# A new instruction order with a refitted plan, first weights loaded by pairs of heads, and q's inverse norm moved into the local exponential

## The chip, the cores and the metric

The kernel runs on one core of one Trainium2 chip. The metric is the device time of one execution in microseconds; the runs of a kernel are summed up by their median.

## The reference

The input is x of shape (8, 512, 128) in fp32: eight independent sequences. Cut to what matters, the reference computes

```python
# 1. causal attention, 16 heads of 64, keys and values shared by pairs of heads
scores = q @ k / 8, causal mask; z = softmax(scores) @ v
x = layernorm(x + z @ W_out + b_out)
# 2. two layers (DEPTH = 2); x1 is the input of the first
for l in range(2):
    h = shift_token(x)                    # second half of the channels one token late
    q, k, v = split(h @ wqkv[l])          # 8 heads of 64
    q = q / |q| * q_scale; k = k / |k| * k_scale     # l2norm per head and token
    q, k = rotary_xpos(q, k)              # also scaled by QK_SCALE = 8
    o = local attention: windows of 64 queries, 128 keys, softmax
    x = x + o @ wo
    h = layernorm(shift_token(x)) * lg + lb
    a, g = split(h @ w1 + b1); x = x + (a * gelu(g)) @ w2 + b2
out = layernorm(x1 + x)
```

The inverse norm of q is one number for each token and head. It is a positive factor of a whole row of scores, so softmax(n * s) can be computed as exp(n * s - max(n * s)) with n applied before the rotary step, or after the scores.

## The kernel before, in words

Everything is fp32, except the mask's small bf16 matmuls. One sequence is held transposed, channels on partitions and 512 tokens along the free axis, in tiles of 128 tokens (NT = 4). The work is written as some 5,900 small operations, each a Python closure with an engine, a planned time and the buffers it reads and writes. `Plan.run` issues them one after the other in `ORDER`, a list of operation numbers written out in the file; each engine gets its instructions in that order. While it does so it keeps a model of the time, and from that model alone it chooses which slot of a buffer class an operation gets: eight PSUM banks, 21 tiles of class `two`, 11 of `four`, 7 of `small` and so on. `HOP` and `TAIL` are the model's delays between an operation and those that wait for it. The waits that the program contains come from the data and the slots; the model's times are not in the program.

Attention (`attention`): for each pair of key heads (`gp`, four of them) `heads` projects keys (L828), queries (L834, two of them) and values (L843); for each of two query heads `results` computes the scores of four query tiles in three groups (L883, two heads side by side on 64 rows each). For each group and head the DVE adds the mask and takes the extreme (`least`, L895), ACT exponentiates with the extreme as a per-partition bias (L907), the DVE inverts the sums (L915), and POOL normalizes (`normalize`, L922). The weights are then transposed on PE (L935, copied back by ACT, L942) or, for most groups of all sequences but the first ("far"), by a DVE transpose in 32 x 32 blocks (L957) and two DMA steps through DRAM (`leave` and `come`, L800 and L804, issued by SP). `values` (L976) multiplies with v on 64 columns for each head, L985 copies back, and `project_out` (L995) adds the heads.

The two layers (`layer`): for each tile of 128 tokens, v (L1033, copied by ACT at L1036 and shifted by windows at L1042 on POOL); q and k (L1056), squared by ACT straight from the bank (L1063), summed by DVE (L1066); the inverse norms by POOL and ACT (L1071, L1077, L1078, and `newton`, L1085 to L1088). The DVE reads the same banks for the rotary step (L1102, L1109), POOL adds the two parts (L1116, 128 x 1024 for q and k together) and multiplies q and k by their inverse norms (`over_norms`, L1122, twice 128 x 512). They are turned by the DVE and DMA (L1156, then SP) or, for the last sequence ("quick"), by PE and ACT (L1136, L1143). Scores of a tile: mask and products in one bank for each parity of heads (L1183, L1198, on quarters of the PE array); for each of the two halves the greatest by DVE (L1219), four exponentials by ACT (L1224), the reciprocals by DVE (L1230), the normalization by POOL (L1232), a transpose on PE (L1239) and a copy by ACT (L1242). Then the outputs (L1251, copied at L1259), wo (L1264), the residual (L1270), layernorm (L754 to L786, L1278), and the gated block (L1288, L1295, L1303, L1306, L1313, L1319). L1328 adds x1, and L1331 stores.

The attention of one sequence and the layers of earlier ones are interleaved in `ORDER`, so that PE has other work while a softmax runs on the other engines. In the plan an operation on PE has one of four tile modes (whole array, rows, columns, quadrants), and a change of mode is planned at 0.1 us. For the last sequence nothing is left to interleave with its second layer.

At the start the loads of `w_k` and `w_v` as a whole and half of `w_q` are issued by ACT's queue (L620 to L623), the other half of `w_q` (`got_q`, L610) and x (L615) by SP's queue, which then issues the tables and the later weights.

Of the kernel before, what the change touches and what calls it, by code (L numbers as in the profile page):

```python
# [12 lines left out]
ALU = mybir.AluOpType  # L13
# [10 lines left out]
class Buf:  # L24


    __slots__ = ("cls", "view", "slot", "t", "left", "free", "marks")

    def __init__(self, cls=None, view=None):
        self.cls, self.view = cls, view  # L30
        self.slot = self.t = None
        self.left = 0
        self.free = 0.0
        self.marks = {}


class Op:
    __slots__ = ("eng", "us", "lat", "fn", "bufs", "mode", "needs", "then", "n", "need", "ready")


class Plan:
# [4 lines left out]
    HOP = (0.055, 0.034, 0.034, 0.085, 0.05)  # L46
# [10 lines left out]
    def op(self, eng, us, fn, r=(), w=(), lat=0.0, hold=(), mode=WHOLE):  # L57
# [33 lines left out]
        o.bufs = bufs  # L91
        self.ops.append(o)

    def run(self, order):
# [6 lines left out]
        for n in order:  # L101
            o = self.ops[n]
            assert not o.need, "an operation stands before one that it needs"
            ready = o.ready
            now = max(at[o.eng], ready)
# [20 lines left out]
            o.fn()  # L126
            for d in o.then:
                d.need -= 1
                d.ready = max(d.ready, end + self.HOP[d.eng])
# [8 lines left out]
    0, 66, 67, 258, 68, 76, 1, 82, 2, 12, 69, 7, 78, 77, 11, 13, 6, 9, 8, 10, 63, 80, 79, 83, 174,  # L138
    175, 187, 200, 194, 259, 808, 81, 215, 188, 16, 176, 177, 201, 195, 228, 241, 189, 207, 208, 32,
    28, 181, 190, 170, 235, 202, 216, 182, 56, 222, 203, 229, 223, 224, 191, 166, 178, 204, 49, 236,  # L140
    19, 183, 209, 184, 179, 210, 74, 171, 237, 180, 14, 196, 242, 230, 168, 72, 185, 225, 211, 3,
    226, 248, 238, 167, 197, 231, 73, 70, 192, 217, 218, 198, 169, 75, 27, 193, 199, 232, 186, 212,
    243, 233, 249, 2262, 219, 71, 220, 205, 206, 221, 172, 234, 173, 213, 244, 239, 250, 245, 240,
    251, 252, 53, 246, 18, 247, 138, 139, 227, 145, 40, 253, 22, 140, 125, 141, 142, 126, 46, 214,
    151, 158, 254, 127, 128, 143, 809, 132, 146, 159, 147, 152, 153, 129, 43, 110, 4, 144, 50, 97,
    160, 161, 148, 84, 154, 64, 111, 262, 104, 133, 134, 21, 155, 130, 135, 255, 47, 98, 85, 149,
    51, 810, 99, 86, 91, 92, 100, 162, 136, 263, 163, 156, 41, 87, 131, 137, 105, 117, 150, 106,
    260, 118, 157, 101, 93, 813, 119, 88, 112, 102, 89, 90, 103, 94, 164, 107, 113, 814, 95, 120,
    121, 122, 114, 115, 116, 108, 292, 165, 96, 52, 299, 109, 266, 293, 300, 267, 301, 294, 268,
    279, 286, 302, 295, 296, 123, 287, 280, 273, 303, 124, 320, 288, 289, 333, 307, 281, 23, 274,  # L150
    304, 269, 20, 270, 282, 327, 25, 297, 334, 335, 321, 322, 290, 291, 314, 275, 323, 283, 5, 276,
    315, 328, 44, 336, 340, 324, 256, 341, 325, 308, 329, 330, 316, 317, 284, 277, 309, 326, 271,
    310, 337, 342, 343, 278, 298, 331, 338, 272, 318, 344, 311, 332, 261, 285, 2989, 257, 305, 319,
    312, 345, 17, 45, 313, 339, 415, 422, 65, 423, 389, 306, 390, 416, 424, 59, 346, 402, 348, 396,
    391, 392, 24, 374, 425, 409, 417, 397, 393, 410, 403, 398, 418, 361, 29, 811, 55, 15, 355, 404,
    347, 349, 399, 419, 57, 362, 411, 412, 356, 357, 358, 405, 394, 264, 350, 375, 406, 413, 351,
    368, 363, 265, 395, 369, 352, 420, 58, 426, 427, 407, 815, 400, 414, 376, 364, 365, 370, 381,
    421, 359, 408, 816, 353, 371, 372, 401, 377, 812, 382, 366, 367, 428, 383, 378, 384, 373, 354,
    379, 380, 385, 61, 360, 62, 839, 844, 840, 386, 387, 827, 832, 866, 429, 388, 841, 878, 845,
    846, 842, 847, 60, 828, 833, 883, 884, 867, 885, 879, 868, 54, 871, 430, 829, 48, 42, 843, 848,  # L160
    872, 830, 1535, 26, 831, 851, 431, 38, 873, 834, 432, 880, 881, 823, 835, 890, 849, 886, 858,
    859, 882, 433, 852, 853, 825, 434, 897, 860, 861, 1536, 874, 909, 824, 898, 1537, 869, 435, 862,
    436, 870, 821, 437, 438, 887, 836, 891, 899, 888, 900, 439, 819, 854, 447, 892, 837, 37, 850,
    838, 875, 445, 893, 826, 855, 894, 876, 901, 456, 455, 453, 820, 454, 457, 910, 485, 889, 863,
    448, 561, 487, 446, 486, 562, 36, 488, 449, 856, 857, 895, 817, 450, 493, 489, 877, 902, 496,
    822, 525, 913, 451, 533, 490, 495, 914, 452, 458, 818, 864, 494, 918, 527, 526, 896, 491, 915,
    865, 937, 916, 497, 459, 919, 925, 944, 460, 920, 903, 534, 945, 930, 926, 528, 529, 563, 921,
    927, 440, 946, 931, 938, 904, 939, 964, 952, 461, 492, 463, 917, 928, 922, 441, 932, 976, 965,
    969, 966, 929, 911, 933, 947, 970, 934, 957, 1540, 530, 531, 566, 958, 977, 912, 907, 498, 948,
    971, 978, 983, 564, 959, 923, 967, 940, 532, 953, 972, 954, 535, 536, 968, 979, 935, 481, 565,  # L170
    905, 949, 2263, 955, 960, 499, 956, 462, 924, 908, 936, 464, 980, 941, 984, 906, 973, 482, 572,
    974, 961, 537, 538, 1541, 471, 567, 568, 942, 981, 569, 521, 943, 985, 950, 982, 465, 2264, 575,
    472, 574, 573, 962, 1001, 986, 473, 474, 1006, 501, 466, 467, 1025, 539, 522, 468, 1013, 951,
    1007, 987, 444, 570, 442, 500, 975, 1032, 995, 443, 963, 988, 484, 1002, 475, 541, 1008, 476,
    1003, 469, 1018, 1019, 1014, 1004, 1015, 1016, 1009, 1005, 1552, 989, 1026, 1020, 503, 470, 996,
    1017, 502, 990, 477, 1021, 1033, 1010, 1052, 540, 1022, 1053, 1034, 543, 1064, 1071, 478, 576,
    1040, 1054, 1057, 1023, 1065, 1058, 504, 511, 1059, 1045, 1538, 542, 1055, 1066, 1041, 571, 577,
    479, 1072, 991, 1073, 1011, 1056, 1027, 1028, 505, 1029, 480, 1042, 1035, 1043, 1067, 1060,
    1046, 1047, 523, 1539, 1061, 578, 1036, 512, 1048, 1074, 993, 1037, 1553, 1030, 994, 544, 513,
    1024, 1044, 1049, 1031, 545, 1012, 524, 483, 506, 551, 1038, 1062, 992, 514, 546, 552, 1079,  # L180
    1080, 1081, 1084, 1103, 553, 1068, 1091, 1085, 580, 507, 1092, 1093, 1050, 1063, 1104, 1082,
    1051, 31, 547, 1086, 1087, 1105, 999, 579, 508, 1546, 35, 515, 1069, 1083, 1110, 1070, 1075,
    997, 582, 1076, 1096, 1106, 1097, 1077, 1000, 516, 509, 1098, 1094, 1095, 1088, 1039, 998, 1118,
    1078, 1142, 510, 1089, 1099, 1100, 1101, 1123, 1130, 1111, 1119, 517, 554, 1124, 1135, 1107,
    1108, 1547, 581, 1112, 1125, 1126, 1136, 1131, 1542, 1113, 1149, 1143, 1120, 1132, 1144, 1543,
    1090, 1724, 555, 1109, 1102, 1121, 1122, 1114, 1133, 1636, 1550, 1137, 30, 1115, 1145, 1134,
    1127, 556, 1128, 1146, 1147, 1138, 1139, 1725, 518, 1148, 1140, 1150, 583, 584, 1116, 1551,
    1554, 590, 1151, 591, 1578, 592, 1555, 1129, 548, 1117, 1566, 1637, 585, 593, 1579, 1152, 1556,
    1634, 1153, 1585, 1544, 1635, 1154, 594, 1141, 1155, 1567, 1568, 586, 1557, 1558, 1559, 1569,
    549, 1605, 1571, 1560, 1572, 1570, 1586, 595, 1561, 1562, 1593, 1563, 1545, 1587, 1573, 1574,  # L190
    1156, 1610, 1575, 1594, 1580, 1617, 550, 587, 1581, 1618, 1588, 1624, 1625, 1598, 1599, 1564,
    1157, 1626, 1576, 39, 1565, 1158, 1582, 1583, 1600, 1595, 1596, 1611, 1589, 1590, 1606, 588,
    1159, 1601, 1612, 519, 1160, 589, 1607, 557, 1584, 596, 1577, 558, 1161, 33, 1597, 1613, 1162,
    1591, 1163, 1691, 1619, 520, 1164, 1608, 1602, 1592, 1627, 1609, 1614, 1603, 1679, 1166, 1615,
    1696, 1165, 1692, 1703, 1680, 597, 1693, 1620, 559, 1174, 1697, 1694, 1684, 1685, 560, 1695,
    1698, 1172, 1173, 1704, 1181, 1621, 1681, 1699, 598, 1175, 1686, 599, 1700, 1604, 1710, 1622,
    1548, 601, 1628, 600, 1167, 602, 1682, 1687, 1182, 1705, 1683, 1616, 1623, 1629, 1183, 603,
    1208, 1180, 1214, 1711, 1688, 1689, 1176, 604, 1712, 605, 1168, 1630, 1549, 1212, 1209, 1184,
    1177, 1631, 1652, 1215, 1701, 1702, 1664, 1640, 1178, 1213, 1653, 1690, 1706, 1654, 606, 1657,
    1179, 1658, 1671, 1672, 1641, 1185, 607, 1659, 1660, 1655, 1642, 1645, 1656, 1632, 1713, 1248,  # L200
# [300 lines left out]
def kernel(  # L501
# [120 lines left out]
    for j in range(2):  # L622
        nc.scalar.dma_start(out=wq_sb[:, :, 1, j, :], in_=wq_v[:, :, 1, j, :])  # L623
# [775 lines left out]
```

## Time and profile before

| | before |
|---|---|
| median of 3 runs | 1193.21 us (1191.84 to 1193.32) |
| the profiled execution | 1189.79 us |
| its span, first to last instruction | 1188.0 us |
| granted clock of PE, share of full speed | 0.997 |
| PE busy | 1154.2 us, 97% |
| DVE, ACT, POOL busy | 952.6, 959.6 and 891.4 us (80%, 81%, 75%) |
| DMA | 173.23 MB, mean 146 GB/s |
| first and last matmul | start at 4.90 us, end at 1180.7 us |

The profiled execution lies 2 us below the fastest of the three runs, so differences are made within the profile and then applied to the median. A row of the groups gives line, engine, operation and tiles, then the busy time and the mean of one instruction in ns, then the idle time of its engine just before it and what ended that. A row of the timeline gives start, length and the merged instructions. Instructions on one engine overlap in part, so the distance from start to start is shorter than the length that is shown.

### The profile page before, as it was taken

To read this page: it belongs to the slowest core of one execution; us is meant where nothing else is said; L and a number is where in the kernel's file an instruction comes from. 1 tells how busy PE (TensorE), PEld (TensorE's weight loads), DVE (VectorE), ACT (ScalarE), POOL (GpSimd) and SP (SyncE) were. 2 spreads that over 40 slices of the span, in tenths; PEclk is the share of its full clock that TensorE was granted. 3 is DMA by queue.
4 is the path that set the end of the run, shared out by engine and by line. 5 is a ranking of instruction groups with operands and counts; after the bars stand their busy time and mean duration, and the time that the engine had idled before them with its cause. 6 is when DMAs were issued, how large, how long until landed. Compare 5 with 4: busy or idle time off the path is not lost.

```text
span 1188.0 us, 32813 instructions
## 1 busy us (share of the span) xinstructions
PE 1154.2 (97%) x11024; PEld 769.2 (65%) x11024; DVE 952.6 (80%) x2988; ACT 959.6 (81%) x3049; POOL 891.4 (75%) x1391
## 2 busy tenths in 40 slices
PE   8999999999999999999999999999999999999986
PEld 5775667566676667666576656766666676666672
DVE  3669967989887989888887888887889888968645
ACT  6867888888888878886898777887788887888783
POOL 3557955789777868778797579786879789989782
PEclk9999999999999999999999999999999999999998
DMA  7004775556655446555556535565456455203100
GB/s 190 15 2 146 241 246 156 178 178 191 196 166 178 162 140 200 174 145 170 160 172 179 188 127 168 159 190 159 157 179 194 136 161 170 81 2 109 36 2 27
DMA packets 180387, 173.23 MB, mean 146 GB/s; under 512 B 25682, under 2 KB 150780, under 8 KB 180220
## 3 DMA queue, kind: packets, MB, share of 16 engines
q1 hardware_dynamic: 178876, 170.35, 46.0%
q8 instruction: 89, 1.46, 0.5%
q10 hardware_dynamic: 1344, 0.79, 0.2%
q14 instruction: 78, 0.64, 0.2%
HBM read 88.22 MB, written 82.84 MB: 144 GB/s over the span
## 4 chain that ended last, share of the span: by engine, by line
PE 75%; DVE 7%; ACT 6%; DMA 4%; POOL 3%; SPq 2%; issue 2%; POOLq 0%; DVEq 0%; ACTq 0%
PE bank L883 11%; PE bank L976 10%; PE bank L1056 6%; PE bank L1251 4%; PE bank L1198 4%; PE bank L995 4%; PE bank L935 4%; PE bank L1264 4%; PE bank L1033 4%; PE bank L1239 4%; PE bank L834 3%; PE bank L1313 3%; PE bank L1303 3%; PE bank L1288 3%; SPq L804 2%
## 5 line engine op out<-in xcount | busy, mean ns | idle before, releaser
L922 POOL TENSOR_SCALAR p<-p,small 128x384 f32<-128x384 f32 (+3 forms) x512 | 264.9, 531 | 123.4 <-DVE small L915 91.8
L1224 ACT ACTIVATE weights<-bank,small 128x128 f32<-128x128 f32 x512 | 181.6, 383 | 27.2 <-DVE small L1219 25.8
L907 ACT ACTIVATE p<-bank,small 128x384 f32<-128x384 f32 (+1 forms) x224 | 142.4, 643 | 29.8 <-DVE small L895 22.4
L1116 POOL TENSOR_TENSOR four<-four,four 128x1024 f32<-128x1024 f32 x64 | 151.4, 2367 | 12.8 <-DVE four L1109 5.4
L1232 POOL TENSOR_TENSOR weights<-weights,small 128x512 f32<-128x512 f32 x128 | 132.3, 1039 | 37.6 <-DVE small L1230 30.3
L883 PE MATMUL bank<-four,four 64*128 64x384 f32 (+3 forms) x1024 | 160.1, 446 | 0.2 <-ACT four L985 0.2
L895 DVE CUSTOM_DVE_ANT_0 bank<-bank,cmask 128x384 f32<-128x384 f32 (+1 forms) x224 | 136.6, 635 | 25.2 <-PE bank L883 24.9
L907 ACT ACTIVATE p<-p,small 128x128 f32<-128x128 f32 (+3 forms) x288 | 135.7, 480 | 15.1 <-DVE small L895 14.8
L1122 POOL TENSOR_TENSOR four<-four,small 128x512 f32<-128x512 f32 x128 | 131.4, 1048 | 2.8
L957 DVE STREAM_TRANSPOSE p<-p 128x768 f32<-128x768 f32 (+1 forms) x112 | 122.4, 1100 | 10.5 <-POOL p L922 10.3
L1056 PE MATMUL bank<-wqkv_sb,hT 128*128 128x512 f32 x256 | 128.3, 601 | 0.2 <-ACT four L1063 0.2
L895 DVE CUSTOM_DVE_ANT_0 p<-bank,cmask 128x256 f32<-128x256 f32 (+3 forms) x288 | 97.4, 380 | 25.2 <-PE bank L883 23.8
L883 PEld LDWEIGHTS bank<-four,four 64*128 64x128 f32 x1024 | 82.8, 186 | 50.9 <-issue 17.1
L1224 ACT ACTIVATION_READ_ACCUMULATOR weights<-bank,small 128x1 f32 x512 | 114.1, 223 | 0.0
L1219 DVE TENSOR_REDUCE small<-bank 128x4 f32<-128x512 f32 x128 | 84.8, 680 | 23.7 <-PE bank L1198 17.6
L1109 DVE TENSOR_TENSOR four<-bank,tb 128x256 f32<-128x256 f32 x256 | 94.6, 414 | 11.4 <-ACT four L1063 6.7
L1102 DVE TENSOR_TENSOR four<-bank,ta 128x512 f32<-128x512 f32 x128 | 85.8, 679 | 13.9 <-ACT four L1063 9.3
L1156 DVE STREAM_TRANSPOSE four<-four 128x512 f32<-128x512 f32 x112 | 92.6, 909 | 2.3 <-POOL four L1122 2.3
L1063 ACT ACTIVATE four<-bank 128x512 f32<-128x512 f32 x128 | 75.4, 610 | 20.2 <-DVE four L1102 7.5
L1242 ACT COPY weights<-bank 128x512 f32<-128x512 f32 x128 | 74.0, 598 | 16.6 <-PE bank L1239 13.6
L1042 POOL COPY two<-two 64x512 f32<-64x512 f32 x128 | 77.2, 606 | 8.9 <-ACT two L1036 2.5
L1066 DVE TENSOR_REDUCE small<-four 128x8 f32<-128x512 f32 x128 | 80.5, 672 | 3.0 <-ACT four L1063 3.0
(104 smaller groups left out, 2692.9 us busy)
## 6 DMA issues: line engine op xcount, KB each, us to landing
dram<-p SPq DMA_DIRECT2D x56, 512.0 KB, 3.4
p4T<-dram SPq DMA_DIRECT2D x224, 128.0 KB, 3.0
dram<-four SPq DMA_DIRECT2D x112, 256.0 KB, 2.8
dram<-p SPq DMA_DIRECT2D x56, 384.0 KB, 2.7
p3T<-dram SPq DMA_DIRECT2D x224, 96.0 KB, 2.8
eight<-dram SPq DMA_DIRECT2D x224, 64.0 KB, 2.2
two<-dram SPq DMA_DIRECT2D x224, 64.0 KB, 2.3
two<-in_L_attn_resid_dram SPq DMA_DIRECT2D x8, 256.0 KB, 3.5
```

Source lines behind the costliest of these rows:

```text
L883: nc.tensor.matmul(s[j].t[:, ds(o, nk)], qT.t[ts(j, E), r, ts(t, P)], kv.t[ts(j, E), 0, :nk], start=True, stop=True,)
L895: nc.vector.tensor_tensor_reduce(s.t[:, :nk] if far else p.t[:, j, ds(o, nk)], s.t[:, ds(o, nk)], cmask[:, S - nk : S], 1.0, 3.0e38, ALU.a ...
L907: nc.scalar.activation(v, negated(p, s, j, o, nk), AF.Exp, bias=st.t[:, 2 * j + i : 2 * j + i + 1], scale=-1.0, accum_out=st.t[:, 8 + 2 * ...
L922: nc.gpsimd.tensor_scalar(v, v, st.t[:, 16 + 2 * j + i : 17 + 2 * j + i], 1.0, ALU.mult, ALU.mult,)
L957: op(DVE, 0.06 + 0.0021 * used, lambda p=p, flat=flat: nc.vector.transpose(flat(p), flat(p)), r=[p], w=[p])
L976: nc.tensor.matmul(pz.t[ts(j, E), ts(t, P)], kv.t[:, 1, ds(kb * P + j * E, E)], turned[:, j, kb] if far else p.t[:, j, ds(POFF[t] - POFF[f ...
L1056: nc.tensor.matmul(pq.t, hT.t[:, ts(t, P)], w if quick else w.rearrange("d (h e b) -> d e h b", e=2, b=B), start=True, stop=True,)
L1109: nc.vector.tensor_tensor(u[:, a], v[:, 1 - a], tb[:, l, t, s, ts(1 - a, B)].unsqueeze(1).broadcast_to([P, H, B]), ALU.mult,)
L1116: op(POOL, 2.35, lambda sw=sw, qn=qn: nc.gpsimd.tensor_tensor(qn.t, qn.t, sw.t, ALU.add), r=[qn, sw], w=[qn])
L1122: nc.gpsimd.tensor_tensor(split(qn.t[:, ts(s, HE)]), split(qn.t[:, ts(s, HE)]), y.unsqueeze(1).unsqueeze(3).broadcast_to([P, 2, H, B]), AL ...
L1224: nc.scalar.activation(weights()[:, c], s.t[:, ts(c, P)], AF.Exp, bias=part(0)[:, c : c + 1], accum_out=part(8)[:, c : c + 1],)
L1232: op(POOL, 1.05, lambda weights=weights, part=part: nc.gpsimd.tensor_tensor(weights(), weights(), spread(part(16)), ALU.mult), r=[(p, j), ...
```

## The change

Five things change in the file.

1. `ORDER` is a new list (6,015 operations for 5,889, as some are split). In the plan, `HOP` is larger (PE 0.1 for 0.055), several planned times are refitted, and a bank remembers who has read or written it and until when (`seen`): an operation of another engine on this bank is planned only after that. `Plan` uses this for its times, and so for the choice of slots.
2. There are 16 slots of class `small` for 7.
3. The first weights are loaded by pairs of heads. ACT's queue loads only the first pair's part of `w_k`, `w_q` and `w_v`; SP's queue loads the rest, eight loads for two, and the projections of a pair wait for their own parts.
4. `over_norms` on POOL treats k alone. q stays without its inverse norm; `greatest` multiplies the negated maximum of the scores (128 x 4) by the norms on the DVE, and the exponential takes the norm as a per-partition `scale` beside its per-partition `bias`. The planned time of the four exponentials stays 1.38.
5. The sum on POOL, and the DVE's transpose of q and k, are planned as two operations, one for q and one for k. The transposes were two instructions already; the sum becomes two.

```diff
-    HOP = (0.055, 0.034, 0.034, 0.085, 0.05)
+    HOP = (0.1, 0.044, 0.044, 0.09, 0.06)
...
+            for b in o.banks:
+                for eng, end in b.seen:
+                    if eng != o.eng:
+                        ready = max(ready, end + self.HOP[o.eng])
...
+            for b in o.banks:
+                b.seen.append((o.eng, end))
...
-    slots("small", [P, 64], 7)
+    slots("small", [P, 64], 16)
...
-    nc.scalar.dma_start(out=wk_sb, in_=w_k)
-    nc.scalar.dma_start(out=wv_sb, in_=w_v)
+    nc.scalar.dma_start(out=wk_sb[:, 0:2, :], in_=w_k[:, 0:2, :])
     for j in range(2):
-        nc.scalar.dma_start(out=wq_sb[:, :, 1, j, :], in_=wq_v[:, :, 1, j, :])
-    got_q = [load(wq_sb[:, :, 0, j, :], wq_v[:, :, 0, j, :], nc.sync) for j in range(2)]
-
+        nc.scalar.dma_start(out=wq_sb[:, 0, :, j, :], in_=wq_v[:, 0, :, j, :])
+    nc.scalar.dma_start(out=wv_sb[:, 0:2, :], in_=w_v[:, 0:2, :])
+    got_q = [[] for gp in range(NGP)]
+    got_q[1] = [
+        load(wk_sb[:, 2:, :], w_k[:, 2:, :], nc.sync), load(wv_sb[:, 2:, :], w_v[:, 2:, :], nc.sync)
+    ]
+    for gp in range(1, NGP):
+        got_q[gp] = got_q[gp] + [
+            load(wq_sb[:, gp, :, j, :], wq_v[:, gp, :, j, :], nc.sync) for j in range(2)]
...
-            op(POOL, 2.35, lambda sw=sw, qn=qn: nc.gpsimd.tensor_tensor(
-                qn.t, qn.t, sw.t, ALU.add), r=[qn, sw], w=[qn])
+            for s in range(2):
+                op(POOL, 1.18, lambda s=s, sw=sw, qn=qn: nc.gpsimd.tensor_tensor(
+                    qn.t[:, ts(s, HE)], qn.t[:, ts(s, HE)], sw.t[:, ts(s, HE)], ALU.add),
+                   r=[(qn, s), (sw, s)], w=[(qn, s)])
...
             def over_norms(sm=sm, qn=qn, split=split):
-                for s in range(2):
-                    y = sm.t[:, ds(32 + s * H, H)]
-                    nc.gpsimd.tensor_tensor(
-                        split(qn.t[:, ts(s, HE)]), split(qn.t[:, ts(s, HE)]),
-                        y.unsqueeze(1).unsqueeze(3).broadcast_to([P, 2, H, B]), ALU.mult,
-                    )
+                k = split(qn.t[:, HE:])
+                nc.gpsimd.tensor_tensor(
+                    k, k, sm.t[:, 32 + H : 32 + 2 * H].unsqueeze(1).unsqueeze(3).broadcast_to(
+                        [P, 2, H, B]), ALU.mult,
+                )
...
-                op(DVE, 0.6, lambda s=s[j], part=part: nc.vector.tensor_reduce(
-                    part(0), by_head(s), AX.X, ALU.max, negate=True), r=[s[j]], w=[(st, j)])
+                def norm_of(c, j=j, sm=sm):
+                    return sm.t[:, 32 + 2 * c + j : 33 + 2 * c + j]
...
+                def greatest(s=s[j], part=part, j=j, sm=sm):
+                    nc.vector.tensor_reduce(part(0), by_head(s), AX.X, ALU.max, negate=True)
+                    nc.vector.tensor_tensor(
+                        part(0), part(0),
+                        sm.t[:, 32 : 32 + H].rearrange("p (c j) -> p j c", j=2)[:, j], ALU.mult)
...
-                            bias=part(0)[:, c : c + 1], accum_out=part(8)[:, c : c + 1],
+                            bias=part(0)[:, c : c + 1], scale=norm_of(c),
+                            accum_out=part(8)[:, c : c + 1],
```

## The prediction

> **What bounds the kernel now.** First the page: busy shares, slices, chain.
>
> ```profile
> PE 1154.2 (97%) x11024; PEld 769.2 (65%) x11024; DVE 952.6 (80%) x2988; ACT 959.6 (81%) x3049; POOL 891.4 (75%) x1391
> PE   8999999999999999999999999999999999999986
> PE 75%; DVE 7%; ACT 6%; DMA 4%; POOL 3%; SPq 2%; issue 2%; POOLq 0%; DVEq 0%; ACTq 0%
> ```
>
> TensorE is the bound: it is idle for 33.8 us of 1188.0. The change removes no matmul, and both programs hold 3266 rows of matmuls in the listing of the order. All it can move is idle time, mode changes and late starts on PE. The windows say where the idle time lies:
>
> ```profile
> core 0: us, PE busy (x) PEld busy (x) DVE busy (x) ACT busy (x) POOL busy (x), PEclk, DMA share, GB/s
> 0.00:30.00 30.00, 24.43 (x143) 15.86 (x145) 11.22 (x53) 18.38 (x50) 9.79 (x26) 1.00 0.78 191
> 30.00:560.00 530.00, 524.73 (x4993) 352.52 (x4991) 439.89 (x1448) 435.70 (x1394) 392.18 (x647) 1.00 0.52 161
> 560.00:1100.00 540.00, 533.41 (x5178) 354.05 (x5174) 453.77 (x1349) 448.97 (x1443) 437.29 (x653) 1.00 0.47 149
> 1100.00:1160.00 60.00, 54.73 (x675) 39.95 (x675) 32.77 (x90) 47.16 (x154) 46.60 (x63) 1.00 0.04 12
> 1160.00:1188.00 28.00, 16.95 (x48) 6.85 (x46) 14.93 (x51) 9.38 (x11) 5.57 (x5) 0.88 0.10 29
> ```
>
> PE's idle time (length less busy time) is 5.6 us in the first stretch, 5.3 and 6.6 in the two long ones, 5.3 while only the last batch is left, and 11.0 in the last 28 us, where one serial chain runs out. But "busy" hides late starts, which the timeline shows:
>
> ```profile
> 641.17 1.02 PE L1033 MATMUL bank<-wqkv_sb,hT 128*128 128x512 f32 x2
> 642.03 1.02 PE L1288 MATMUL bank<-two,w_sb 128*128 128x512 f32 x2
> 642.99 0.88 PE L976 MATMUL bank<-p,four 128*64 128x128 f32 x12
> ...
> 654.66 1.06 PE L1264 MATMUL bank<-two,wo_sb 128*128 128x128 f32 x8
> 655.63 3.70 PE L995 MATMUL bank<-four,wout_sb 128*128 128x512 f32 x8
> ```
>
> From start to start the L1033 pair takes 0.86 us. The same pair of L1288 takes 0.96, because the next operation uses another tile mode (L976, 64 columns): a mode change costs 0.10 us. The eight of L1264 take 0.97 where most of their kind take 0.89, without a mode change: the next operation's operand came too late to be prepared. I took all 1265 steps from one PE operation to the next, each against the shortest usual step (the 5th percentile) of its kind with the same kind of mode change. The excess is **67 us**, 17.5 of it recorded as waits. 416 steps exceed by over 20 ns. Where the last release before a late step lies within 0.4 us (43 us of the 67), it comes from ACT in 24 us, DVE in 9, POOL in 8, DMA in 2. So PE is tightly fed, most often at the last moment by ACT.
>
> **The change part by part.** The profiled execution took 1189.79 us around its span of 1188.0; the median of the runs is 1193.21, 3.4 above it. I work out a difference on the profile and apply it to the median.
>
> *New order, mode changes.* Counting in the two listings, PE changes its tile mode 381 times before and 408 times after. 27 x 0.095 us (between the 0.05 of some steps out of L1251 and the 0.10 above) is **+2.6 us**, all on PE.
>
> *New order, late data.* The new order comes from refitted costs: PE now sees an operand 0.10 us after its release where the plan had 0.055, and readers of one bank on ACT and DVE exclude each other in the plan. I counted how much PE work (durations of the trace) stands between a producer and its consumer. From attention's scores to the transposes of their weights (through DVE, ACT, POOL): under 5 us 7 times before, 2 after; under 7 us 24 and 16. From scores to values through the two DMAs: under 24 us 34 times and 30. From the local transposes to the local outputs, through one ACT copy: under 1.5 us 13 and 8. Against it: attention's transposes to values under 1.5 us 11 times and 18; local outputs to wo under 2.5 us 11 and 18. More gets room than loses it. Bounds: 0 (queues behind other work set the lateness, not distance) and two thirds of the 43 us, -29. I take a third, **-15 us**, since the classes point both ways.
>
> *q's norm in the exponential, ACT.* The 512 exponentials (L1224) get a second per-partition operand, the scale. The rows next to it:
>
> ```profile
> L1224 ACT ACTIVATE weights<-bank,small 128x128 f32<-128x128 f32 x512 | 181.6, 383 | 27.2 <-DVE small L1219 25.8 <-DVE small L915 0.9
> L1063 ACT ACTIVATE four<-bank 128x512 f32<-128x512 f32 x128 | 75.4, 610 | 20.2 <-DVE four L1102 7.5 <-PE bank L1056 5.6 <-DVE four L1109 3.2
> L1295 ACT ACTIVATE hid<-bank,b_sb 128x512 f32<-128x512 f32 x32 | 20.0, 675 | 0.2 <-PE bank L1288 0.2
> L1278 ACT ACTIVATE two<-bank,bb_sb,g_sb 128x512 f32<-128x512 f32 x16 | 12.8, 797 | 2.2 <-PE bank L786 2.0
> ```
>
> At one size: no such operand 610 ns, a bias 675, bias and scale 797. Back to back, L1063 starts every 493 ns and L1295 every 585. So a scale costs 65 to 122 ns; I take 0.092, the step between starts. That is 0.37 us for the four of a half tile and 47 us of ACT in all, 81% to 85%. The plan still books 1.38 us for the four, what they take now (starts 0.342 apart), so its order gives them no room. Behind them in ACT's queue stand bank copies that PE waits for. ACT idles 214 us in 476 gaps, half of them under 0.2 us, so a delay of 0.37 often outlives the next gap. PE's share of the 47 us lies between none and half (+24). I take a sixth, **+8 us**: ACT ends a late step in about a twelfth of PE's steps, and I double it because each delay meets several of ACT's outputs.
>
> The Trainium skill speaks against this part: the page "ScalarE: Activation LUTs", section "What ACT_TABLE_LOAD costs", says each per-partition pointer operand adds about 93 ns to an ACTIVATE. By that price it would be 48 us of ACT, as by the rows.
>
> *The same, POOL and DVE.* POOL loses q's half of L1122, 64 x 1.048 = 67 us; splitting L1116 (2.367) costs at most 64 x (2 x 1.273 - 2.367) = 11 us (1.273 is L1328, of half size). POOL goes to some 832 us, 70%. Two long stretches hide it, where POOL ends 8 us of late steps, 3.0 of them at the very end in L1328, which stays. In 1100 to 1160 it shows: four L1116 and eight L1122 take 17.7 us there, and the chain of waits passes through them. Half of the four q halves (4.2 us) is **-2.5 us** with the little inside; bounds 0 and -5.3, PE's whole idle time in that stretch.
>
> DVE gains 128 small multiplies: 128 x 0.166 us (L1230, the same shape) = 21 us, 80% to 82%, and 0.1 to 0.17 us stands between maximum and exponential, of which the plan books 0.06. It can be late for PE as now: **+1 us**, bounds 0 and +4. The maximum also reads the norms now; newton on POOL wrote them before k's rotated tile, which the scores need anyway, so this wait ends earlier. It would hold DVE's queue otherwise, and with it the banks of attention's scores.
>
> *First weights by pairs.* PE starts at 4.90 us, when x lands; then a copy on ACT. The first six L828 matmuls take 4.85 us where two usually take 0.86, starts 0.85 apart, though the granted clock reads 1.00: a slow beginning that six projections fill in either order. No wait for a weight is recorded. On SP six more issues of about 0.6 us stand before the rotary tables and the later weights; their first reader waits at 12.2 us on POOL and the first local layer comes after 170 us, so they are hidden. If that cover were gone it would be 3.6 us. **0**, bounds -1 (x landed in 4.04 us against a median of 3.5, with less beside it) and +1. The turned halves (L1156, 909 ns) stay two instructions, their DMAs are as many, and the larger pool of small tiles can only free: 0.
>
> Sum: 2.6 - 15 + 8 - 2.5 + 1 + 0 = -5.9. **1187.3 us**.
>
> **The rivals.** *ACT is late* (0.25): half of the 47 us reaches PE: 2.6 - 15 + 24 - 2.5 + 1 = +10, 1203. For it speaks ACT as the first among the late releasers and the unchanged 1.38; against it 214 us of ACT idle time. It decides from a share of 0.30 on, where the sum is nought.
>
> *The order brings nothing* (0.15): lateness stays, 2.6 + 8 - 2.5 + 1 = +9, 1202. For it speaks that the distances point both ways.
>
> *Two thirds go* (0.10): -29 with ACT's +8 gives -20, 1173; for it the attention distances.
>
> *The bank rule does nothing* beyond its order: the program already makes readers of one bank wait (L1063 behind L1102, 7.5 us, above); the new lines only move planned times and the choice of a slot. It lies inside the cases.
>
> **How the numbers follow.** The forecast has 0.50, its own range 1180 to 1191. A measurement here tells apart about 0.2%, 2.4 us. Faster: 0.45 of the forecast and the 0.10. Within: 0.05 of the forecast, 0.05 of ACT, 0.02 of the third. Slower: the other 0.33. The range 1173 to 1203 leaves out half of the best case and about 0.12 above.
>
> **What would show it.** The exponentials (L1254 in the new listing) should run at 450 to 500 ns, its starts 0.43 apart; ACT near 1005 us, POOL near 832, DVE near 973. PE's late steps should fall from 67 us to about 60 with ACT's share risen; its idle time in the long stretches should not grow; the stretch of the last batch should lose 2 us. A start of the attention scores later than 14.1 us would make the first stretch wrong. Late steps above 75 us, released by ACT, would make the prediction wrong by the first rival; late steps below 45 would mean that ACT's extra work is free.

## The result, and the profile after

The changed kernel takes **1219.53 us** (median of 4 runs, 1218.39 to 1221.71) against 1192.53 (4 runs, 1188.90 to 1193.32) of the kernel before on the same chip: a ratio of 1.0235, interval 1.0208 to 1.0261, so slower by 25 to 31 us. The forecast of 1187.3 had the wrong sign, and its range of 1173 to 1203 does not hold the time. The profiled execution took 1220.23 us, with a span of 1218.2 and a granted clock of 0.994.

First the page after: busy shares, the slices of PE, the chain by engine.

```profile
PE 1171.3 (96%) x11024; PEld 769.9 (63%) x11024; DVE 995.4 (82%) x3116; ACT 1003.8 (82%) x3049; POOL 836.9 (69%) x1391
PE   8999999999999999999999999999999999999985
PE 46%; ACT 12%; DVE 9%; issue 3%; POOL 2%; DMA 1%; SPq 0%; POOLq 0%; DVEq 0%; ACTq 0%
```

PE still issues 11024 matmuls and its slices still read 9, so the shares alone would call this kernel as well fed as before. But PE's busy time grew by 17 us with the same matmuls, so part of the loss hides in busy time, as late starts did before the change. The chain that ended last was followed back over 73% of the span here (the sum of its parts) and 99% before; of what was followed, PE has 63% for 75, and ACT and DVE together 29% for 13. ACT is at 1003.8 and POOL at 836.9, as forecast; DVE is at 995.4 where 973 was forecast. That surplus of 22 us is the first trace of what went wrong.

The windows of the changed kernel show that the loss is spread and not at one place:

```profile
core 0: us, PE busy (x) PEld busy (x) DVE busy (x) ACT busy (x) POOL busy (x), PEclk, DMA share, GB/s
0.00:30.00 30.00, 24.95 (x144) 15.49 (x144) 10.13 (x51) 18.67 (x51) 13.51 (x36) 1.00 0.69 174
30.00:560.00 530.00, 519.76 (x4843) 345.28 (x4844) 445.71 (x1461) 443.18 (x1376) 358.30 (x619) 1.00 0.50 159
560.00:1100.00 540.00, 528.91 (x5141) 347.94 (x5139) 468.80 (x1407) 459.18 (x1402) 397.20 (x642) 1.00 0.48 148
...
1160.00:1190.00 30.00, 26.93 (x312) 19.55 (x312) 13.25 (x58) 25.58 (x75) 17.63 (x24) 1.00 0.00 1
1190.00:1219.00 29.00, 14.90 (x37) 6.48 (x36) 13.60 (x43) 7.06 (x9) 5.56 (x5) 0.78 0.10 27
```

PE's idle time in the two long stretches is 10.2 and 11.1 us where it was 5.3 and 6.6, and fewer matmuls fit into each: 4843 and 5141 for 4993 and 5178. With the count of the prediction (each step on PE against the 5th percentile of its kind) the change in span divides as follows:

| us | before | after | change |
|---|---|---|---|
| first matmul starts | 4.90 | 4.27 | -0.6 |
| the steps at their shortest | 1108.0 | 1110.5 | +2.5 |
| late steps | 67.1 | 95.0 | +27.9 |
| of these, last release by ACT | 24.4 | 41.9 | +17.5 |
| by DVE | 8.6 | 13.1 | +4.5 |
| by POOL | 8.4 | 6.3 | -2.1 |
| released by the local exponentials' line | 2.3 | 21.2 | +18.9 |

The first three sum, by the way they are made, to the start of PE's last step: it came 29.8 us later, and the span grew by 30.2. So the loss lies along PE's whole work, most of it in late steps, and two thirds of their growth ends at one line of ACT. The split is good to a few us only: if neighbouring operations of one kind are taken as one step, the same traces give 60.7 and 84.8 us of late steps and +6.2 for the steps at their shortest. The waits of PE that the profile records name the same line:

```profile
engine line waited for: us in total, times, longest us
...
PE bank L907 <- ACT weights L1254: 3.8, 7, 1.1
PE bank L1270 <- ACT weights L1254: 2.6, 6, 0.8
...
PE bank L1319 <- ACT weights L1254: 1.9, 2, 1.4
...
PE bank L1057 <- ACT weights L1254: 1.4, 2, 0.9
```

L907 (attention's scores), L1057 (v) and L1319 (the gated block) read nothing that the local exponentials write. What they can want of them is a PSUM bank: the exponentials are the last to read the scores' banks, and a bank that comes free later holds up whatever PE operation gets it next. ACT's other lines release as much late work as before (20.7 us for 22.1). The groups of the changed part:

```profile
L1254 ACT ACTIVATE weights<-bank,small,small 128x128 f32<-128x128 f32 x512 | 228.0, 469 | 31.9 <-DVE small L1246 26.2 <-DVE small L939 2.3 <-PE bank L907 1.6
L1245 DVE TENSOR_REDUCE small<-bank 128x4 f32<-128x512 f32 x128 | 86.6, 677 | 15.8 <-PE bank L1220 15.5
L1246 DVE TENSOR_TENSOR small<-small,small 128x4 f32<-128x4 f32 x128 | 43.6, 340 | 4.7
L1140 POOL TENSOR_TENSOR four<-four,four 128x512 f32<-128x512 f32 x128 | 162.5, 1274 | 16.9 <-DVE four L1125 8.0 <-DVE four L1132 5.4 <-DVE small L939 1.7
```

The exponential takes 469 ns for 383, within the forecast 450 to 500. The small multiply (L1246), forecast at 166 ns, takes 340 ns on the mean.

Three theories stood at this point. **A**: the scale operand makes ACT late, the prediction's first rival; the sign that the prediction gave for it, late steps above 75 us released by ACT, is there. **B**: the new order is itself worse and the norm has little to do with it. **C**: the small multiply between maximum and exponential costs more than its price.

### The profile page after: what moved, and what is told of

The parts are those of the page before. It is cut to its first block, busy times and chain, and to the rows that moved or that the text cites. A ratio compares the mean times of both kernels' runs of the same rounds, so it can differ in the third digit from the quotient of the medians.

```text
span 1218.2 us, 32947 instructions
## 1 busy us (share of the span) xinstructions
PE 1171.3 (96%) x11024; PEld 769.9 (63%) x11024; DVE 995.4 (82%) x3116; ACT 1003.8 (82%) x3049; POOL 836.9 (69%) x1391
## 4 chain that ended last, share of the span: by engine, by line
PE 46%; ACT 12%; DVE 9%; issue 3%; POOL 2%; DMA 1%; SPq 0%; POOLq 0%; DVEq 0%; ACTq 0%
ACT weights L1254 8%; PE bank L907 6%; PE bank L1079 5%; PE bank L1000 4%; PE bank L1220 3%; PE bank L1282 3%; PE bank L1270 3%; PE bank L1295 3%; PE bank L1334 3%; PE bank L1319 2%; PE bank L1057 2%; PE bank L1344 2%; PE bank L1019 2%; DVE small L1245 2%; PE bank L858 2%
## 5 line engine op out<-in xcount | busy, mean ns | idle before, releaser
L946 POOL TENSOR_SCALAR p<-p,small 128x512 f32<-128x512 f32 (+3 forms) x512 | 265.2, 531 | 163.4 <-DVE small L939 130.3
L1254 ACT ACTIVATE weights<-bank,small,small 128x128 f32<-128x128 f32 x512 | 228.0, 469 | 31.9 <-DVE small L1246 26.2
L1140 POOL TENSOR_TENSOR four<-four,four 128x512 f32<-128x512 f32 x128 | 162.5, 1274 | 16.9 <-DVE four L1125 8.0
L931 ACT ACTIVATE p<-bank,small 128x512 f32<-128x512 f32 (+1 forms) x224 | 142.3, 642 | 35.5 <-DVE small L919 25.3
L907 PE MATMUL bank<-four,four 64*128 64x512 f32 (+3 forms) x1024 | 165.5, 450 | 5.2 <-ACT weights L1254 3.8
L919 DVE CUSTOM_DVE_ANT_0 bank<-bank,cmask 128x512 f32<-128x512 f32 (+1 forms) x224 | 136.7, 634 | 26.5 <-PE bank L907 24.9
L931 ACT ACTIVATE p<-p,small 128x256 f32<-128x256 f32 (+3 forms) x288 | 136.5, 485 | 7.7 <-DVE small L919 7.4
L1079 PE MATMUL bank<-wqkv_sb,hT 128*128 128x512 f32 x256 | 128.9, 607 | 1.8 <-ACT weights L1254 0.6
L907 PEld LDWEIGHTS bank<-four,four 64*128 64x128 f32 x1024 | 82.7, 186 | 61.0 <-issue 16.3
L1254 ACT ACTIVATION_READ_ACCUMULATOR weights<-bank,small,small 128x1 f32 x512 | 110.4, 216 | 0.0
L1245 DVE TENSOR_REDUCE small<-bank 128x4 f32<-128x512 f32 x128 | 86.6, 677 | 15.8 <-PE bank L1220 15.5
L959 PEld LDWEIGHTS bank<-ident,p 128*128 128x128 f32 x496 | 57.3, 141 | 44.7 <-issue 23.8
L966 ACT COPY p<-bank 128x384 f32<-128x384 f32 (+1 forms) x136 | 66.1, 499 | 21.7 <-PE bank L959 20.5
```

What stands on the lines that cost most here:

```text
L907: nc.tensor.matmul(s[j].t[:, ds(o, nk)], qT.t[ts(j, E), r, ts(t, P)], kv.t[ts(j, E), 0, :nk], start=True, stop=True,)
L919: nc.vector.tensor_tensor_reduce(s.t[:, :nk] if far else p.t[:, j, ds(o, nk)], s.t[:, ds(o, nk)], cmask[:, S - nk : S], 1.0, 3.0e38, ALU.a ...
L931: nc.scalar.activation(v, negated(p, s, j, o, nk), AF.Exp, bias=st.t[:, 2 * j + i : 2 * j + i + 1], scale=-1.0, accum_out=st.t[:, 8 + 2 * ...
L946: nc.gpsimd.tensor_scalar(v, v, st.t[:, 16 + 2 * j + i : 17 + 2 * j + i], 1.0, ALU.mult, ALU.mult,)
L1079: nc.tensor.matmul(pq.t, hT.t[:, ts(t, P)], w if quick else w.rearrange("d (h e b) -> d e h b", e=2, b=B), start=True, stop=True,)
L1140: op(POOL, 1.18, lambda s=s, sw=sw, qn=qn: nc.gpsimd.tensor_tensor(qn.t[:, ts(s, HE)], qn.t[:, ts(s, HE)], sw.t[:, ts(s, HE)], ALU.add), r ...
```

## The experiments

**Taking the two added costs away, one at a time and together, in the new order.** e1 keeps the multiply (by ones) and drops the scale operand, e2 keeps a scale operand (of ones) and drops the multiply, e3 drops both. So e1 to e3 leave q's norm out of the result. e4 goes the other way: the norm in the exponential, in the old order, with the whole result.

```diff
 # e1
-    sm.t[:, 32 : 32 + H].rearrange("p (c j) -> p j c", j=2)[:, j], ALU.mult)
+    ones, ALU.mult)
-    bias=part(0)[:, c : c + 1], scale=norm_of(c),
+    bias=part(0)[:, c : c + 1],
 # e2
-    nc.vector.tensor_tensor(part(0), part(0), ..., ALU.mult)
-    bias=part(0)[:, c : c + 1], scale=norm_of(c),
+    bias=part(0)[:, c : c + 1], scale=ones[:, 0:1],
 # e3
-    nc.vector.tensor_tensor(part(0), part(0), ..., ALU.mult)
-    bias=part(0)[:, c : c + 1], scale=norm_of(c),
+    bias=part(0)[:, c : c + 1],
 # e4, in the kernel before
-    for s in range(2):          # over_norms
+    for s in (1,):
+    ... greatest, norm_of and scale=norm_of(c) as in the changed kernel
```

> The changed kernel, its order and all else as it is, but the exponentials take no scale operand (q's inverse norm is left out of the computation; the small multiply on the DVE stays, by ones). Theory A, ACT's second operand is the cause: the exponentials fall from 469 to about 383 ns, ACT to about 958 us, the late steps on PE behind the exponentials from 21 to about 3 us, and the time from 1219.5 to 1196 to 1202 us. Theory B, the new order itself is worse: ACT falls as well, but the time stays at 1212 us or more. Theory C, the small multiply on the DVE is the cause: 1215 us or more.

> The changed kernel without the small multiply on the DVE after the maximum (q's inverse norm is left out; the exponentials keep a scale operand, of ones). Theory A: DVE falls by about 44 us of busy time, the chain before the exponentials by 0.3 us, and the time by 3 to 6 us, to 1213 to 1217. Theory B: within 2 us of 1219.5. Theory C: 1205 us or less.

> The changed kernel with neither the scale operand nor the small multiply (q's inverse norm is left out altogether, so POOL is relieved of it for nothing): the new order by itself. Theory A: 1188 to 1196 us, the late steps on PE at 60 to 67 us. Theory B: 1208 us or more. If the new order is as much better as was forecast for it (15 us less of late data), 1180 to 1186.

> The kernel before, its order and its loads, with q's inverse norm moved from POOL into the exponential as in the change (16 small tiles). Theory A: the cost comes with the move and not with the order, so 1208 to 1218 us, with ACT near 1005 us. Theory B, the order is the cause: 1190 to 1198 us.

| | median us | ratio to before | interval | late steps us | by the exponentials |
|---|---|---|---|---|---|
| after | 1219.53 | 1.0235 | 1.0208 to 1.0261 | 95.0 | 21.2 |
| e1, no scale | 1193.29 | 1.0028 | 1.0018 to 1.0038 | 68.5 | 5.2 |
| e2, no multiply | 1198.41 | 1.0072 | 1.0057 to 1.0087 | 73.4 | 11.7 |
| e3, neither | 1177.49 | 0.9889 | 0.9874 to 0.9904 | 51.7 | 2.6 |
| e4, norm in the old order | 1247.82 | 1.0476 | 1.0458 to 1.0493 | 128.9 | 29.3 |

The kernel before took 1190.14 us beside e1 to e4. B falls: without the norm's two costs the new order is 12.7 us faster than before, and with them the old order is far worse than the new one. A and C both hold, and neither alone: e1 came out below the 1196 to 1202 us that A expected, e2 below its 1213 to 1217, and e4 far above its 1208 to 1218. On top of e3 the scale alone costs 20.9 us, the multiply alone 15.8, and both together about 41 (0.0346 of 1190); some 5 of these belong to neither alone. The rows of the multiply (e1) and of the exponentials (e1, e2, e3):

```profile
L1248 DVE TENSOR_TENSOR small<-small,ones 128x4 f32<-128x4 f32 x128 | 46.5, 363 | 4.4
L1254 ACT ACTIVATE weights<-bank,small 128x128 f32<-128x128 f32 x512 | 181.8, 379 | 36.1 <-DVE small L1248 31.6 <-DVE small L941 2.4 <-DVE small L1261 1.1
```

```profile
L1253 ACT ACTIVATE weights<-bank,small,ones 128x128 f32<-128x128 f32 x512 | 228.5, 475 | 16.3 <-DVE small L1247 14.8 <-PE bank L1002 0.7
```

```profile
L1251 ACT ACTIVATE weights<-bank,small 128x128 f32<-128x128 f32 x512 | 181.8, 383 | 16.4 <-DVE small L1245 14.3 <-PE bank L1000 0.7 <-DVE small L939 0.3
```

The two costs enter ACT by different doors. The scale makes the exponentials themselves longer (46 us more busy time) and leaves the wait ahead of them as it was, 16 us. The multiply leaves their length and doubles that wait to 36 us: ACT stands at an exponential until the DVE has multiplied, everything behind it in its queue stands too, and the scores' bank is held for as long.

**The same two costs in the old order, and the multiply with another operand.** e5 adds only a scale of ones to the kernel before, e6 only a multiply by ones; both keep the whole result. e7 asks why the multiply is so long. Theory **D** of the expectations: a DVE instruction with two operands in SBUF is held until POOL's running instruction ends. In e7 the second operand is a row of scores in PSUM in place of the norms in SBUF, and the operation is a comparison. A softmax does not depend on what is subtracted from all of its scores, so the exponential's bias may be that value; what e7 leaves out is the greatest as the shift.

```diff
 # e5, in the kernel before
-    bias=part(0)[:, c : c + 1], accum_out=...
+    bias=part(0)[:, c : c + 1], scale=ones[:, 0:1], accum_out=...
 # e6, in the kernel before, after the maximum
+    nc.vector.tensor_tensor(part(0), part(0), ones, ALU.mult)
 # e7, in the changed kernel
-    nc.vector.tensor_tensor(part(0), part(0), sm.t[:, 32 : 32 + H]..., ALU.mult)
+    nc.vector.tensor_tensor(part(0), part(0), by_head(s)[:, :, 0], ALU.is_ge)
```

> The kernel before, its order and POOL's norms as they are, with one thing added: the exponentials take a scale operand, of ones. Theory A (a delay of ACT of 0.37 us for each half tile reaches PE by half, in either order): ACT near 1005 us, the time 20 to 28 us above before, 1210 to 1218. If only the new order is sensitive: within 8 us of before.

> The kernel before with the small multiply on the DVE added after the maximum, by ones. Theory D, a DVE instruction with two operands in SBUF waits until POOL's running instruction has ended: its mean is 350 to 550 ns with lengths that follow POOL's, and the time is 18 to 32 us above before. If its own work is the cost: 165 ns throughout and 3 us or less.

> The changed kernel with the small DVE instruction reading its second operand from the scores' bank in PSUM in place of the norms in SBUF (a comparison in place of the product, so the bias is not the right one; the same count, shape and place). Theory D: it takes 160 to 190 ns throughout and the time falls by most of what leaving it out gave (21 us), to 1199 to 1206. If it is the place in the chain or the instruction that costs: 1215 or more.

| | median us | ratio to before | interval | late steps us |
|---|---|---|---|---|
| e5, scale, old order | 1212.26 | 1.0181 | 1.0158 to 1.0204 | 90.5 |
| e6, multiply, old order | 1228.07 | 1.0319 | 1.0297 to 1.0340 | 102.4 |
| e7, multiply from PSUM, new order | 1206.78 | 1.0142 | 1.0123 to 1.0161 | 81.6 |

The kernel before took 1190.12 us here. The scale costs 22.1 us in the old order and 20.9 in the new one: its price hardly depends on the order. The multiply costs 37.9 us in the old order, more than D's 18 to 32, and 15.8 in the new one. In the old order the two prices sum to 60 us, and e4, which has both and relieves POOL, stands 57.7 above before. The rows of the multiply, e6 first, then e7 with its exponentials:

```profile
L1223 DVE TENSOR_TENSOR small<-small,ones 128x4 f32<-128x4 f32 x128 | 67.6, 528 | 4.4
```

```profile
L1246 DVE TENSOR_TENSOR small<-small,bank 128x4 f32<-128x4 f32 x128 | 20.2, 158 | 4.4
L1253 ACT ACTIVATE weights<-bank,small,small 128x128 f32<-128x128 f32 x512 | 228.3, 470 | 22.2 <-DVE small L1246 16.5 <-PE bank L907 2.2 <-PE bank L1281 1.2
```

128 instructions of the same shape take 67.6, 43.6 or 20.2 us, by what stands beside them and where an operand lies. In e7 every one of them takes 157 to 159 ns, although 100 of them start while POOL is at work, and ACT's wait before the exponentials falls from 31.9 to 22.2 us. In the changed kernel the 34 that start while POOL is idle take 161 to 166 ns; the 23 that start during the sum of L1140 have a median of 586. The timeline of the changed kernel shows one, DVE and POOL alone:

```profile
315.27 0.68 DVE L1245 TENSOR_REDUCE small<-bank 128x4 f32<-128x512 f32 x1
315.70 1.27 POOL L1140 TENSOR_TENSOR four<-four,four 128x512 f32<-128x512 f32 x1
315.98 1.01 DVE L1246 TENSOR_TENSOR small<-small,small 128x4 f32<-128x4 f32 x1
```

The maximum, which reads PSUM, is not disturbed as POOL begins (677 ns is the mean of its row). The multiply, four elements a partition, starts at 315.98 and ends at 316.99; POOL's sum ends at 316.97. Over the cases of this kind, its length is what is left of POOL's instruction plus some 20 ns: 427 ns with 407 left, 624 with 603, 586 with 567. The Trainium skill states this on the page "SBUF — State Buffer", section "Who interferes with whom": a DVE instruction with two SBUF inputs takes turns with a GpSimd instruction that reads SBUF, and the later one is held until the other has ended. The runs agree with it but for one group: beside POOL's powers of L793 (6 cases, POOL still busy for 141 to 555 ns) the multiply takes at most 164 ns. All six begin 481 ns or more after the power began, so its first part is not tested.

In the changed kernel e7's edit gains 12.7 us of the 21 that dropping the multiply (with a scale kept, e2) gains. So about 60% of the multiply's price is the hold by POOL. The other 8.4 us, the distance from e2 to e7, go with an instruction of 158 ns: one more dependent step between maximum and exponential. In the old order the hold is longer because POOL's instructions are: there the sum is one instruction of 2.4 us, and of the 18 multiplies that met it the median is 1590 ns. How much of the larger price there comes from the longer hold, and how much from the order, no run separates. The split of that sum into two, which the prediction booked as a small cost to POOL, goes with a shorter hold of the DVE; no run has the split alone.

**The new order with q's norm on POOL as before.** e8 wanted the order without the norm's costs and with the whole computation: neither scale nor multiply, and a POOL operation for q's norm issued as soon as its inputs are there, ahead of those that need it.

```diff
+    def over_norms_q(sm=sm, qn=qn, split=split):
+        q = split(qn.t[:, :HE])
+        nc.gpsimd.tensor_tensor(q, q, ..., ALU.mult)
+    op(POOL, 1.0, over_norms_q, r=[(qn, 0), sm], w=[(qn, 0)], extra=True)
```

> The changed kernel with q's inverse norm back on POOL: its order, loads, banks and split sums, no scale operand, no small multiply; q's multiply follows as soon as the norms and q's sum are there, and the few operations that stood before it are put behind it. The new order without norms took 1177.5 us, 13 below before. POOL gets 67 us back (some 905 us, 76%), as before the change. Theory A and D: 1179 to 1188 us, faster than both kernels. If the relief of POOL was what made the new order fast: 1190 or more.

It took 1280.69 us, ratio 1.0764 (1.0742 to 1.0786), against 1190.12 and an expected 1179 to 1188: a clear miss. The waits of its DVE point to the cause:

```profile
DVE four L1195 <- POOL four L1162: 68.5, 37, 5.5
DVE small L1261 <- PE bank L1236: 25.7, 25, 3.6
```

The new list places the DVE's transposes of q (L1195) early, since no norm stood before them. With the norm back on POOL, the DVE stands at the head of its queue for 68.5 us until it comes. So the order seems to fit only the program that it was made for; PE's own waits in e8 were not taken apart. What an order made anew with the norm on POOL would give stays open; e3 shows only what the order gives without q's norm at all.

**What is left if the maximum goes, and the other parts alone.** e9 keeps the scale, and drops maximum, multiply and bias. It computes the same softmax: the scale operand makes q's length one inside the exponential, so that what is exponentiated stays at most about 8 times the learned scales, which are 1 in this input; with learned scales far above 1 the exponential would overflow. e10 takes q's norm from POOL in the old order and puts it nowhere. e11 has the new first loads in the old order.

```diff
 # e9, in the changed kernel
-    nc.vector.tensor_reduce(part(0), by_head(s), AX.X, ALU.max, negate=True)
-    nc.vector.tensor_tensor(part(0), part(0), ..., ALU.mult)
-    bias=part(0)[:, c : c + 1], scale=norm_of(c),
+    scale=norm_of(c),
 # e10, in the kernel before
-    for s in range(2):          # over_norms
+    for s in (1,):
 # e11, in the kernel before
+    ... the first pair's weights on ACT's queue, the rest on SP's behind x
```

> The changed kernel without the local maximum: no reduction, no small multiply and no bias; the exponentials keep the norm as their scale. Softmax is the same for any bias of a row, and the scores of normalized q and k stay far from overflow in this input; for larger scales this would not be safe. If the two costs found so far are the whole story (a second operand on ACT, a DVE step that waits for POOL), this has neither: exponentials at about 383 ns, DVE near 870 us, and 1160 to 1178 us, under the 1177.5 of the new order without norms and faster than both kernels. If the exponentials still cost 470 ns (a bias is brought as an operand anyway): 1185 to 1200.

> The kernel before, its order, with q's inverse norm left out altogether: POOL loses the 67 us and nothing takes their place. It parts the 13 us by which the new order without norms beats before into POOL's relief and the order. If the order makes it: 1186 to 1191 us. If the relief of POOL makes it: 1176 to 1181.

> The kernel before with the change's first loads alone (the first pair of heads on ACT's queue; the rest behind x on SP's). x lands earlier in all runs with these loads: the first matmul starts at 4.2 to 4.3 us where it starts at 4.9 to 5.3 with the old ones. If PE's whole work moves with it: 0.3 to 1.0 us faster than before. If the second pair's weights come late, which this order wants first: up to 3 us slower.

| | median us | ratio to before | interval |
|---|---|---|---|
| e9, no maximum | 1177.10 | 0.9896 | 0.9879 to 0.9912 |
| e10, POOL's relief, old order | 1188.92 | 0.9992 | 0.9983 to 1.0001 |
| e11, new loads, old order | 1188.44 | 0.9991 | 0.9981 to 1.0002 |

The kernel before took 1190.30 us here. e10 and e11 can't be told from no change: POOL's relief is worth -2.0 to +0.1 us, the loads -2.3 to +0.2. In e11 the first matmul starts at 4.28 us where it was 4.90 before (and 5.21 in e10, with the old loads), so if there is a gain, x landing earlier would account for it; the interval holds zero. e9 is faster than both kernels, by 1.0% and 3.3% (0.9896 over 1.0235), and level with e3. Its page and its exponentials:

```profile
PE 1151.1 (98%) x11024; PEld 768.1 (65%) x11024; DVE 879.3 (75%) x2860; ACT 958.8 (81%) x3049; POOL 836.6 (71%) x1391
L1251 ACT ACTIVATE weights<-bank,small 128x128 f32<-128x128 f32 x512 | 181.5, 389 | 3.3 <-DVE two L1298 1.5 <-PE bank L1220 1.1 <-ACT weights L1270 0.3
```

With one pointer operand the exponential takes 389 ns, whether that is the bias (383 before) or the scale: so the price goes with each operand. And 75 us less DVE work than e3 (879.3 for 954.6) and 13 us less waiting on ACT (3.3 for 16.4) brought nothing beyond e3. Once PE's late steps are down to 55.5 us (51.7 in e3), more room on DVE and ACT is not what PE lacks.

## Why the prediction was wrong, point by point

*What bounds the kernel.* It held. PE's late steps were the quantity to watch, ACT was first among the releasers, and PE's last step came 29.8 us later with a span longer by 30.2.

*Mode changes, +2.6.* Right in the count: the traces too have 381 and 408 changes of the tile mode. The steps at their shortest grew by 2.5 us, which agrees, though that figure is good to a few us only (+6.2 with steps cut otherwise).

*The new order's late data, -15.* Right in size: 51.7 us of late steps in e3 for 67.1, -15.4, of which POOL's relief has 1.7 by e10's 65.4. This third of the 43 us was a choice between far bounds, so its closeness is partly luck. The rival "the order brings nothing" falls by e3.

*ACT's scale operand, +8.* The work was right: 86 ns each forecast as 92, 44 us in all by busy time (1003.8 less 959.6). The page "ScalarE: Activation LUTs" of the Trainium skill, section "What ACT_TABLE_LOAD costs", has about 93 ns, and agrees. **The share that reaches PE was the failed step.** A sixth was taken; measured are 20.9 us on top of e3, 22.1 in the old order, and 25 to 26 from the changed kernel to e1, so about half. The reasoning "ACT ends a late step in a twelfth of PE's steps, doubled" counted the steps that were late already. A longer ACT instruction also makes steps late that had been in time: with neighbouring operations of one kind taken as one step, 397 steps are late by over 20 ns before, and 458 in e5, which adds nothing but the scale. The prediction had the warning itself, 214 us of idle time on ACT in 476 gaps of which half are under 0.2 us, and then took the smaller share. e2, which is the change with the scale but without the multiply, stands 8.3 us above before; the first rival's sum without its +1 for DVE is +9. That rival was right for its part.

*DVE's small multiply, +1 with bounds 0 to +4.* **The second failed step, and the one that left its own bounds.** Measured: +15.8 on top of e3, 21 from the changed kernel to e2. Either cost alone would have stayed in the range of 1173 to 1203 (e1 1193.29, e2 1198.41); the two together left it. It was priced by a reciprocal of the same shape (166 ns), which reads one operand. The row's form `small<-small,small` has two, both in SBUF. So the nearest row was not near: the shape agreed, but the number of SBUF operands did not, and POOL beside it was left out. At 340 ns instead of 166 it is longer by 22 us of DVE, which is the surplus over the forecast 973. The rest of the error is the place: even at 158 ns the step cost 8.4 us (e7 against e2), so slack on the engine that runs it did not hide a step between two waiting engines. The term assumed that the DVE "can be late for PE as now", while the one who waited was ACT (31.6 us on the multiply in e1), with its queue and a bank behind it.

*POOL, -2.5.* The sign may hold; e10 gives -1.4, interval -2.0 to +0.1. The end did not gain 2 us: the late steps from 1100 us on rose from 14.7 to 22.0, though the longer span puts a little more work behind that mark.

*First weights, 0.* Within its bounds: the first matmul came 0.6 us earlier, and e11 gives -2.3 to +0.2 us, which does not settle more.

*The sum with the measured terms.* 2.5 - 15.4 - 0.6 for the order with POOL's relief and the loads gives -13.5 (e3: -12.7); 20.9 for ACT, 15.8 for the multiply, some 5 for the two together: +28, and +27 was measured between the medians. The two failed terms were booked at 9 us and cost about 41.

## What to carry to other kernels

The uncertain term is "work on an engine that is not the bound, times the share of it that reaches the bound". Here, where the bounding engine is often fed at the last moment, that share was about half in both orders of the work; where nothing else is known, half is a better first guess than a sixth. Before pricing a new DVE instruction by a row of the same shape, count its operands in SBUF, and look at how long POOL's instructions beside it are; and price a step inserted between two engines at the queue of the one that waits. When work is moved to engines with idle time, also ask whether the operation that it serves is needed: here the kernel without the maximum (e9) was 3.3% faster than the changed one, at the price of no guard against overflow.

## What the runs showed of the hardware

A 128x4 multiply on the DVE, two operands in SBUF, took 161 to 166 ns with POOL idle and up to 1.5 us in the changed kernel, 2.9 us in the old order; a comparison of the same shape with one operand in PSUM took 157 to 159 ns in all 128 cases of e7. One of 1503 ns began with 247 ns left of POOL's instruction and ended 25 ns after the end of POOL's next one, so it was held through both. What POOL computes matters too: beside its powers on 128x4 the 6 multiplies of the changed kernel that began in the second part of a power were not held (at most 164 ns). In the record of the trace the hold is part of the DVE instruction's length and not idle time ahead of it, so it shows as a busy DVE and in no list of waits.
